# Two graph-attention layers on one core: layer-1 and layer-2 scores from extra weight columns, rows spread through DRAM, and a bfloat16 adjacency load

## The chip, the cores and the metric

The kernel runs on one core of a Trainium2 chip. Times are device microseconds (us) of that core. A profiled execution has a span (first to last instruction) and a time that also holds what lies around it.

## The reference

There are 32 samples, each with 512 nodes of 512 features and a 512x512 adjacency matrix of 0 and 1. Two blocks follow each other; each normalises the rows, applies ReLU, runs a graph attention and adds the result to its input.

```python
# layer 0 (one head): i attends to its neighbours j
s = s_src[i] + s_dst[j] + b;  e = leaky_relu(s, 0.2);  e = where(adj + eye == 0, -inf, e)
x = x + softmax(e, axis=j) @ h
# layer 1, gat_layer twice: 4 heads of 256, elu, then 1 head of 512
xl = x @ W;  asrc = einsum(xl, a_src);  adst = einsum(xl, a_dst)      # one number per node and head
e = leaky_relu(asrc[s] + adst[d], 0.2);  e = where(adj > 0 or s == d, e, -1e9)
out[d] = sum_s softmax(e, axis=s) * xl[s] + bias
```

Everything is computed in float32. In this text, layer 1 is the first `gat_layer` (four heads) and layer 2 the second (one head).

## The kernel before

A sample's 512 nodes are four tiles of 128 partitions (`T` = 4). All of a sample stays in SBUF. The program is written with tile pools; a scheduler decides the order of the instructions on each engine, and every engine runs its instructions in that order. A tile of a pool with `bufs` slots has to wait until the slot's last user is done.

An attention has these steps, and all of them appear in layer 0, in each of the four heads of layer 1 and in layer 2:

- **Projection** (`layer1_project`, L307; `layer2_project`, L383): products of 128 nodes by 512 columns, each accumulated over the contraction in PSUM, copied to SBUF by ACT (L311, L387). Layer 1 takes two heads at once.
- **Scores** (`dot`, L165): VectorE multiplies a row of features with an attention vector and sums, for source and target. The result is a column, one number per node: a and c.
- **Spread** (`spread`, L152): a column must lie along the free dimension, the same on all partitions. Four TensorE transposes, one per node tile, write it to a PSUM tile `row` of 128x512.
- **Maxima** (`neighbour_max`, L173): per node tile, VectorE adds the additive mask (0 or -2^100) to the row of a and takes the maximum. Then `shifts` works out, in tiny VectorE operations (L180 to L185), the two columns p and q. They contain the softmax's shift.
- **Edge weights** (`edge_weights`, L188 to L199): p and q are spread. Per node tile of 128x512: ACT computes q + 0.2 a (L195), VectorE max(p + a, that) (L196), POOL adds the mask (L197), ACT takes Exp (L198).
- **Aggregation** (`aggregate`, L206): TensorE multiplies the edge weights with the values and a column of ones, so that the sum of weights comes along. VectorE divides (L217 to L219, L345 to L346).

Layer 1's heads go through ELU (L352, L353) and are transposed for layer 2 (`layer1_head_T`, L366, L367).

The masks (`masks0`, `masks1`) come from the int32 adjacency tile on VectorE (L231 to L248), and are also transposed on TensorE (L160, L161). Layer 0's normalised rows are transposed in `layer1_in` (L160).

The main loop (L415) is software-pipelined: in step b it projects sample b for layer 1, aggregates layer 2 of sample b-1 (`layer2_out`), works out all four heads' maxima (`layer1_shifts`), then runs layer 0's aggregation of sample b+1 (`layer0_out`) and `layer1_in(b+1)`, the four heads of sample b with the next head's edge weights ahead of each, `layer2_project(b)`, and the masks, load and scores of samples b+1 and b+2. SP issues the loads of x and adj and the store of out; the constants are loaded from ACT's queue ahead of the loop. PSUM's eight slots are divided as `p_acc` 3, `p_tr` 2 and `p_bc` 3 (the rows).

Of the kernel before, what the change touches and what calls it, by code (L numbers as in the profile page):

```python
# [15 lines left out]
P = 128  # L16
# [8 lines left out]
def kernel(  # L25
# [32 lines left out]
    NW = 2 * H  # L58
# [13 lines left out]
    p_acc = ctx.enter_context(tc.tile_pool(name="p_acc", bufs=3, space=PSUM))  # L72
    p_tr = ctx.enter_context(tc.tile_pool(name="p_tr", bufs=2, space=PSUM))
    p_bc = ctx.enter_context(tc.tile_pool(name="p_bc", bufs=3, space=PSUM))
# [7 lines left out]
    def load_adj(b: int):  # L82
        A[b] = big.tile([P, T, N], I32, tag="adj", name=f"adj_{b}")
        nc.sync.dma_start(A[b], node_tiles(adj, b))
# [22 lines left out]
    w1_s = const.tile([P, KD, HF], F32, name="w1_s")  # L107
    w2_s = const.tile([P, KH, D], F32, name="w2_s")
    nc.scalar.dma_start(w1_s, w1.rearrange("(k p) f -> p k f", p=P))

    att1_r = const.tile([P, 2, HF], F32, name="att1_r")
    att2_r = const.tile([P, 2, D], F32, name="att2_r")
# [3 lines left out]
    def load_constants():  # L116
        for i, (a1, a2) in enumerate(((att_src1, att_src2), (att_dst1, att_dst2))):
            nc.scalar.dma_start(att1_r[:, i, :], rows(a1, HF))
            nc.scalar.dma_start(att2_r[:, i, :], rows(a2, D))
        nc.scalar.dma_start(b1_r, rows(b1, HF))  # L120
        nc.scalar.dma_start(b2_r, rows(b2, D))
        nc.scalar.dma_start(w2_s, w2.rearrange("(k p) f -> p k f", p=P))

        nc.vector.tensor_scalar(b1_r, b1_r, 1.0, None, op0=ALU.add)

# [22 lines left out]
    def spread(col_of):  # L148

        row = p_bc.tile([P, N], F32, tag="bc", name="row")  # L150
        for t in range(T):
            nc.tensor.transpose(row[:, node_block(t)], col_of(t).to_broadcast([P, P]), ident)  # L152
        return row
# [15 lines left out]
    def neighbour_max(amax, h, mask, row):  # L169

        for t in range(T):
            junk = work.tile([P, N], BF16, tag="junk", name="junk_m")
            nc.vector.tensor_tensor_reduce(  # L173
                junk, mask[:, t, :], row, 1.0, LOWEST, ALU.add, ALU.max, accum_out=amax[:, t, h : h + 1]
            )

    def shifts(c, amax, heads, name):

        z = cols.tile([P, T, heads], F32, tag=f"z{name}", name=f"z{name}")
        nc.vector.tensor_add(z, c, amax)  # L180
        m = cols.tile([P, T, heads], F32, tag=f"m{name}", name=f"m{name}")
        nc.vector.scalar_tensor_tensor(m, z, SLOPE, z, op0=ALU.mult, op1=ALU.max)  # L182
        pq = cols.tile([P, 2, T, heads], F32, tag=f"pq{name}", name=f"pq{name}")
        nc.vector.tensor_sub(pq[:, 0], c, m)
        nc.vector.scalar_tensor_tensor(pq[:, 1], c, SLOPE, m, op0=ALU.mult, op1=ALU.subtract)  # L185
        return pq

    def edge_weights(name, tag, pq, h, a_of, a2_of, mask):  # L188

        E = big.tile([P, T, N], F32, tag=tag, name=name, bufs=2)  # L190
        p_row = spread(lambda t: pq[:, 0, t, h : h + 1])
        q_row = spread(lambda t: pq[:, 1, t, h : h + 1])
        for t in range(T):
            e = E[:, t, :]
            nc.scalar.activation(e, q_row, AF.Identity, bias=a2_of(t), scale=1.0)  # L195
            nc.vector.scalar_tensor_tensor(e, p_row, a_of(t), e, op0=ALU.add, op1=ALU.max)  # L196
# [14 lines left out]
    def attend(E, values, xt):  # L211

        for t in range(T):
            hi = aggregate(E, t, lambda s: values[:, s, HD : D + 1])
# [9 lines left out]
    M = {}  # L224
# [30 lines left out]
    def layer0_scores(b: int):  # L255
# [4 lines left out]
        c = cols.tile([P, T, 1], F32, name="c0")  # L260
        a = cols.tile([P, T, 1], F32, name="a0")
        for t in range(T):
            relu_normed(h0[:, t, :D], xt, t, rstd, nmr)
            dot(h0[:, t, :D], ws_r, c[:, t, :])
            dot(h0[:, t, :D], wd_r, a[:, t, :])
        nc.vector.tensor_scalar(c, c, b0_r, None, op0=ALU.add)  # L266
        a2 = cols.tile([P, T, 1], F32, name="a20")
        nc.vector.tensor_scalar(a2, a, SLOPE, None, op0=ALU.mult)
        m0, m0T = masks0(b)
        amax = cols.tile([P, T, 1], F32, name="amax0")  # L270
        neighbour_max(amax, 0, m0, spread(lambda t: a[:, t, :]))
        pq = shifts(c, amax, 1, "0")
        L0[b] = (h0, edge_weights(f"E0_{b}", "E_one", pq, 0, lambda t: a[:, t, :], lambda t: a2[:, t, :], m0T))
# [23 lines left out]
    def layer1_project(b: int):  # L297
        hT = HT.pop(b)
        ac = cols.tile([P, T, NW], F32, name="ac1")

        xl = [big.tile([P, T, 2, F + 1], F32, tag="pair", name=f"xl_{b}_{i}", bufs=3) for i in range(PAIRS)]
        for i in range(PAIRS):
            nc.gpsimd.memset(xl[i][:, :, :, F : F + 1], 1.0)  # L303
            for t in range(T):
                acc = p_acc.tile([P, 512], F32, tag="acc", name="acc")
                for k in range(KD):
                    nc.tensor.matmul(  # L307
                        acc, hT[:, k, node_block(t)], w1_s[:, k, i * 512 : (i + 1) * 512],
                        start=(k == 0), stop=(k == KD - 1),
                    )  # L310
                nc.scalar.copy(xl[i][:, t, :, :F], acc.rearrange("p (h f) -> p h f", f=F))  # L311
                for j in range(2):
                    h = 2 * i + j
                    for side in range(2):
                        n = side * H + h
                        dot(xl[i][:, t, j, :F], att1_r[:, side, h * F : (h + 1) * F], ac[:, t, n : n + 1])
        L1[b] = (ac, xl)

    def layer1_shifts(b: int):
        ac, xl = L1[b]  # L320
        m1T = M[b][1]
        a2 = cols.tile([P, T, H], F32, name="a21")
        nc.vector.tensor_scalar(a2, ac[:, :, :H], SLOPE, None, op0=ALU.mult)
        amax = cols.tile([P, T, H], F32, name="amax1")
        for h in range(H):
            neighbour_max(amax, h, m1T, spread(lambda t: ac[:, t, h : h + 1]))
        pq = shifts(ac[:, :, H:], amax, H, "1")
        L1[b] = (ac, a2, pq, xl)
# [3 lines left out]
    def layer1_head_scores(b: int, h: int):  # L332
        ac, a2, pq, _ = L1[b]
        return edge_weights(
            f"E_{b}_{h}", "E", pq, h, lambda t: ac[:, t, h : h + 1], lambda t: a2[:, t, h : h + 1], M[b][0]
        )

    def layer1_head(b: int, h: int, E):

        xl = L1[b][3][h // 2]  # L340
        v = work.tile([P, T, F], F32, tag="v", name=f"v_{b}_{h}")
        for t in range(T):
            acc = aggregate(E, t, lambda s: xl[:, s, h % 2, :])
# [28 lines left out]
    def layer2_project(b: int):  # L372
# [4 lines left out]
        xl = big.tile([P, T, D + 1], F32, tag="xl2", name=f"xl2_{b}")  # L377
        nc.gpsimd.memset(xl[:, :, D : D + 1], 1.0)
        ac = cols.tile([P, T, 2], F32, name="ac2")
        for t in range(T):  # L380
            acc = p_acc.tile([P, 512], F32, tag="acc", name="acc")
            for k in range(KH):
                nc.tensor.matmul(  # L383
                    acc, h1T[k // per][:, k % per, node_block(t)], w2_s[:, k, :],
                    start=(k == 0), stop=(k == KH - 1),
                )
            nc.scalar.copy(xl[:, t, :D], acc)  # L387
            for side in range(2):
# [80 lines left out]
```

## Time and profile before

| | us |
|---|---|
| three runs | 4755.22, 4755.69, 4651.54 (median 4755.22) |
| the profiled execution, its time | 4652.77 |
| the profiled execution, its span | 4651.0 |
| TensorE busy with products | 4210.5 (91%) |
| VectorE busy | 2918.1 (63%) |
| ACT busy | 1841.0 (40%) |
| POOL busy | 1134.8 (24%) |

An fp32 product or transpose is one row of the program; a product's record in the trace is one of its two passes. In a row of the groups, the columns are: line, engine, operation, out<-in with shapes, count; then busy time in us and the mean in ns of one; then the idle time of the engine just before these instructions and what ended it. In a timeline the idle time stands in square brackets with what ended it. PEclk is the granted TensorE clock as a share of full speed. In the list of DMA issues, the last number is the median time from issue to landing, in us.

The chain of work that ended last gives 69% of the span to TensorE, 20% to VectorE, 4% to POOL and 4% to ACT.

### The profile page before, as it was taken

How to read it: one execution, taken by the hardware profiler on the slowest of the kernel's cores; microseconds unless marked ns; L12 is line 12 of the kernel's file. 1: busy time of each engine (PE TensorE's matmuls, PEld its weight loads, DVE VectorE, ACT ScalarE, POOL GpSimd, SP SyncE). 2: the span in 40 equal slices, each digit the busy share in tenths (PEclk: the TensorE clock that was granted, in tenths of full speed). 3: DMA queues.
4: the chain of work that ended last, by engine and by line, in shares of the span. 5: the costliest groups of instructions: out<-in, count | busy, mean ns of one | idle time of the engine just before them, and what ended most of it. 6: DMA issues, size and time to landing. Idle time of an engine off the chain costs nothing.

```text
span 4651.0 us, 49799 instructions
## 1 busy us (share of the span) xinstructions
PE 4210.5 (91%) x17152; PEld 2844.0 (61%) x17152; DVE 2918.1 (63%) x9029; ACT 1841.0 (40%) x3073; POOL 1134.8 (24%) x1094
## 2 busy tenths in 40 slices
PE   6998899898998989999889989899898999989997
PEld 4566656666565665656656566656566565665665
DVE  6656665567666576665666656766657666576644
ACT  2434324434344343343432444424434334343343
POOL 1322212223122232132321322212223213232121
PEclk9999999999999999999999999999999999999998
DMA  3000000000000000000000000000000000000000
GB/s 115 10 19 28 28 28 10 19 27 28 28 19 19 19 28 28 28 10 19 28 28 28 10 19 28 28 28 13 24 19 28 28 28 10 19 28 28 10 1 19
DMA packets 53802, 110.92 MB, mean 24 GB/s; under 512 B 1840, under 2 KB 1840, under 8 KB 53552
## 3 DMA queue, kind: packets, MB, share of 16 engines
q1 hardware_dynamic: 50688, 100.67, 6.2%
q10 hardware_dynamic: 2864, 7.08, 0.4%
q8 instruction: 137, 2.24, 0.2%
q14 instruction: 113, 0.93, 0.1%
HBM read 74.19 MB, written 33.55 MB: 23 GB/s over the span
## 4 chain that ended last, share of the span: by engine, by line
PE 69%; DVE 20%; POOL 4%; ACT 4%; issue 2%; DMA 0%; POOLq 0%; SPq 0%; ACTq 0%; DVEq 0%
PE acc L206 31%; PE acc L383 19%; PE acc L307 12%; DVE junk_m L173 7%; DVE junk L165 4%; POOL E L197 4%; DVE E L196 3%; PE pt L366 2%; PE pt L160 2%; ACT hn L146 2%; PE row L152 2%; DVE x L219 1%; DVE d L235 1%; POOL rstd L140 1%; DVE c L266 1%
## 5 line engine op out<-in xcount | busy, mean ns | idle before, releaser
L206 PE MATMUL acc<-xl,E 128*128 128x257 f32 (+1 forms) x6144 | 1420.0, 387 | 58.8 <-DVE v L346 53.3
L206 PEld LDWEIGHTS acc<-xl,E 128*128 128x128 f32 x6144 | 1158.3, 192 | 258.7 <-issue 72.4
L165 DVE SCALAR_TENSOR_TENSOR junk<-xl,att_r 128x256 bf16<-128x256 f32 (+1 forms) x1280 | 604.7, 524 | 765.4 <-ACT xl L387 750.1
L195 ACT ACTIVATE E<-row,a 128x512 f32<-128x512 f32 x768 | 478.8, 684 | 1256.3 <-PE row L152 1197.0
L197 POOL TENSOR_TENSOR E<-E,m 128x512 f32<-128x512 f32 x640 | 747.8, 1193 | 752.6 <-DVE E L196 750.3
L307 PE MATMUL acc<-w_s,hT 128*128 128x512 f32 x2048 | 922.3, 597 | 0.0
L383 PE MATMUL acc<-w_s,h1T 128*128 128x512 f32 x2048 | 894.8, 592 | 0.0
L383 PEld LDWEIGHTS acc<-w_s,h1T 128*128 128x128 f32 x2048 | 381.7, 190 | 443.9 <-issue 443.9
L206 PE MATMUL acc<-h,E 128*128 128x257 f32 (+1 forms) x2048 | 510.1, 408 | 134.1 <-DVE m L182 128.8
L196 DVE SCALAR_TENSOR_TENSOR E<-row,ac,E 128x512 f32<-128x512 f32 x640 | 452.0, 744 | 276.5 <-ACT E L195 276.4
L307 PEld LDWEIGHTS acc<-w_s,hT 128*128 128x128 f32 x2048 | 372.6, 191 | 385.3 <-issue 377.1
L198 ACT ACTIVATE E<-E 128x512 f32<-128x512 f32 x768 | 479.6, 628 | 272.6 <-POOL E L197 269.9
L206 PEld LDWEIGHTS acc<-h,E 128*128 128x128 f32 x2048 | 415.3, 207 | 209.3 <-issue 140.4
L173 DVE CUSTOM_DVE_ANT_0 junk_m<-m1T,row 128x512 bf16<-128x512 bf16 x640 | 394.1, 682 | 0.0
L387 ACT COPY xl<-acc 128x512 f32<-128x512 f32 x128 | 75.1, 587 | 741.2 <-PE acc L383 741.2
L219 DVE SCALAR_TENSOR_TENSOR x<-acc,r,x 128x256 f32<-128x256 f32 x512 | 246.4, 482 | 176.7 <-PE acc L206 169.4
L353 DVE SCALAR_TENSOR_TENSOR v<-e,v 128x512 f32<-128x512 f32 x256 | 178.1, 696 | 237.3 <-ACT e L352 237.3
L303 POOL MEMSET xl<- 128x8 f32 x64 | 7.1, 112 | 1053.1 <-PE acc L383 795.9
L152 PE MATMUL row<-ident,pq 128*128 128x128 f32 x1536 | 210.8, 278 | 43.2 <-ACT E L195 31.2
L140 POOL TENSOR_TENSOR rstd<-ve,minus_half 128x4 f32<-128x4 f32 x64 | 64.0, 1013 | 754.1 <-DVE ve L138 754.1
L311 ACT COPY xl<-acc 128x512 f32<-128x512 f32 x256 | 148.9, 582 | 244.4 <-PE acc L307 244.4
L346 DVE SCALAR_TENSOR_TENSOR v<-acc,r,b_r 128x256 f32<-128x256 f32 x512 | 238.9, 482 | 10.3
(64 smaller groups left out, 3262.1 us busy)
## 6 DMA issues: line engine op xcount, KB each, us to landing
x<-in_x_dram SPq DMA_DIRECT2D x32, 1024.0 KB, 5.1
adj<-in_adj_dram SPq DMA_DIRECT2D x32, 1024.0 KB, 5.2
out_dram<-x SPq DMA_DIRECT2D x32, 1024.0 KB, 4.3
w_s<-in_L_gnn_W_dram ACTq DMA_DIRECT2D x2, 2048.0 KB, 13.7
att_r<-in_L_gnn_att_src_dram ACTq DMA_DIRECT2D x1, 512.0 KB, 17.3
att_r<-in_L_gnn_att_dst_dram ACTq DMA_DIRECT2D x1, 512.0 KB, 7.4
b_r<-in_L_gnn_b_dram ACTq DMA_DIRECT2D x1, 512.0 KB, 9.5
ws_r<-in_L_gnn_attn_w_src_dram ACTq DMA_DIRECT2D x1, 256.0 KB, 5.2
```

Source lines behind the costliest of these rows:

```text
L152: nc.tensor.transpose(row[:, node_block(t)], col_of(t).to_broadcast([P, P]), ident)
L165: nc.vector.scalar_tensor_tensor(junk[:, : vector.shape[1]], values, 1.0, vector, op0=ALU.mult, op1=ALU.mult, accum_out=out)
L173: nc.vector.tensor_tensor_reduce(junk, mask[:, t, :], row, 1.0, LOWEST, ALU.add, ALU.max, accum_out=amax[:, t, h : h + 1])
L195: nc.scalar.activation(e, q_row, AF.Identity, bias=a2_of(t), scale=1.0)
L196: nc.vector.scalar_tensor_tensor(e, p_row, a_of(t), e, op0=ALU.add, op1=ALU.max)
L197: nc.gpsimd.tensor_add(e, e, mask[:, t, :])
L198: nc.scalar.activation(e, e, AF.Exp)
L206: nc.tensor.matmul(out, E[:, s, node_block(t)], values(s), start=(s == 0), stop=(s == T - 1))
L219: nc.vector.scalar_tensor_tensor(xt[:, t, f], acc[:, :HD], r, xt[:, t, f], op0=ALU.mult, op1=ALU.add)
L307: nc.tensor.matmul(acc, hT[:, k, node_block(t)], w1_s[:, k, i * 512 : (i + 1) * 512], start=(k == 0), stop=(k == KD - 1),)
L346: nc.vector.scalar_tensor_tensor(v[:, t, :], acc[:, :F], r, b1_r[:, h * F : (h + 1) * F], op0=ALU.mult, op1=ALU.add)
L383: nc.tensor.matmul(acc, h1T[k // per][:, k % per, node_block(t)], w2_s[:, k, :], start=(k == 0), stop=(k == KH - 1),)
```

## The change

Four things are edited.

1. The weights of layer 1 and layer 2 get two more columns per head, W times a_src and W times a_dst. They are worked out once on VectorE, in the prologue. The projection then yields a and c itself, so the dots over the projected rows are gone. Layer 1's projection is now one head per product (258 columns); layer 2's is two products of 257 columns.
2. `spread` no longer transposes a broadcast column per tile into PSUM. One transpose turns the 4 columns of a (or the 8 of p and q) into 4 (8) partitions, ACT copies them to SBUF, SP stores them to a DRAM tile, and SP loads them from there onto all 128 partitions. The row tiles are now in SBUF, two slots for a and two for p with q. PSUM's slots are redivided as `p_acc` 5 and `p_tr` 3.
3. adj is loaded as bfloat16 by POOL's DMA queue, in place of int32 by SP's.
4. `layer1_project` and `layer1_shifts` go head by head, each head's shifts (with its maxima) behind the next head's projection. The last head's shifts stand behind `layer2_out`. `layer0_out(b+1)` and `layer1_in(b+1)` are moved from ahead of the heads to behind them.

The core of the diff:

```diff
-    p_acc = ctx.enter_context(tc.tile_pool(name="p_acc", bufs=3, space=PSUM))
-    p_tr = ctx.enter_context(tc.tile_pool(name="p_tr", bufs=2, space=PSUM))
-    p_bc = ctx.enter_context(tc.tile_pool(name="p_bc", bufs=3, space=PSUM))
+    p_acc = ctx.enter_context(tc.tile_pool(name="p_acc", bufs=5, space=PSUM))
+    p_tr = ctx.enter_context(tc.tile_pool(name="p_tr", bufs=3, space=PSUM))
+    dram = ctx.enter_context(tc.tile_pool(name="dram", bufs=4, space=bass.MemoryType.DRAM))
...
     def load_adj(b: int):
-        A[b] = big.tile([P, T, N], I32, tag="adj", name=f"adj_{b}")
-        nc.sync.dma_start(A[b], node_tiles(adj, b))
+        A[b] = big.tile([P, T, N], BF16, tag="adj", name=f"adj_{b}")
+        nc.gpsimd.dma_start(A[b], node_tiles(adj, b))
...
+        for h in range(H):
+            for k in range(KD):
+                for i in range(2):
+                    dot(w1_s[:, k, h, 2:], att1_r[:, i, h * F : (h + 1) * F], w1_s[:, k, h, i : i + 1])
+        for k in range(KH):
+            for i in range(2):
+                dot(w2_s[:, k, 2:], att2_r[:, i, :], w2_s[:, k, i : i + 1])
...
-    def spread(col_of):
-        row = p_bc.tile([P, N], F32, tag="bc", name="row")
-        for t in range(T):
-            nc.tensor.transpose(row[:, node_block(t)], col_of(t).to_broadcast([P, P]), ident)
+    def spread(col, n, tag, bufs):
+        pt = p_tr.tile([P, N], F32, tag="tr", name="pt_row")
+        nc.tensor.transpose(pt[: n * T, :P], col, ident)
+        line = cols.tile([n * T, P], F32, tag=f"line{n}", name="line")
+        nc.scalar.copy(line, pt[: n * T, :P])
+        there = dram.tile([n * T, P], F32, tag=f"there{n}", name="there")
+        nc.sync.dma_start(there, line)
+        row = big.tile([P, n, N], F32, tag=tag, name=tag, bufs=bufs)
+        nc.sync.dma_start(row, there.rearrange("r p -> (r p)").partition_broadcast(P).rearrange("q (n m) -> q n m", n=n))
         return row
...
+    def shift_rows(a, c, mask):
+        a_row = spread(a, 1, "a_row", 2)
...
+        neighbour_max(amax, mask, a_row[:, 0, :])
...
+        return a2, spread(pq.rearrange("p r t -> p (r t)"), 2, "pq_row", 2)
...
-            nc.scalar.activation(e, q_row, AF.Identity, bias=a2_of(t), scale=1.0)
-            nc.vector.scalar_tensor_tensor(e, p_row, a_of(t), e, op0=ALU.add, op1=ALU.max)
+            nc.scalar.activation(e, rows_pq[:, 1, :], AF.Identity, bias=a2[:, t : t + 1], scale=1.0)
+            nc.vector.scalar_tensor_tensor(e, rows_pq[:, 0, :], a[:, t : t + 1], e, op0=ALU.add, op1=ALU.max)
             nc.gpsimd.tensor_add(e, e, mask[:, t, :])
             nc.scalar.activation(e, e, AF.Exp)
...
+    def layer1_project(b: int, h: int):
...
+                nc.tensor.matmul(
+                    acc[:, : 2 + F], HT[b][:, k, node_block(t)], w1_s[:, k, h, :],
...
+            nc.scalar.copy(xl[:, t, h % 2, : 2 + F], acc[:, : 2 + F])
...
+            accs = [p_acc.tile([P, 512], F32, tag="acc", name="acc") for _ in range(2)]
             for k in range(KH):
...
+                for i in range(2):
+                    nc.tensor.matmul(
+                        accs[i][:, :W], h1T[k // per][:, k % per, node_block(t)], w2_s[:, k, i * W : (i + 1) * W],
...
         if b < B:
-            layer1_project(b)
+            for h in range(H):
+                layer1_project(b, h)
+                if h:
+                    layer1_shifts(b, h - 1)
...
-        layer1_shifts(b)
-        if b + 1 < B:
-            layer0_out(b + 1)
-            layer1_in(b + 1)
+        layer1_shifts(b, H - 1)
...
         layer1_head_T(b, H - 1)
+        if b + 1 < B:
+            layer0_out(b + 1)
+            layer1_in(b + 1)
         layer2_project(b)
```

## The prediction

> **What bounds the kernel now.** I read the table of stages over one sample first (from one layer-2 aggregation at 1949.00 us to the next at 2092.36), then TensorE's timeline inside it, then the groups by shape.
>
> ```profile
> core 0: us, PE busy (x) PEld busy (x) DVE busy (x) ACT busy (x) POOL busy (x), PEclk, DMA share, GB/s
> 1949.00:2092.36 143.36, 131.11 (x538) 88.63 (x537) 91.22 (x283) 57.45 (x96) 35.49 (x34) 0.98 0.06 23
> ```
>
> 32 periods of 143.36 us make 4587.5 of the 4651.0 us span; 63.5 us lie ahead and behind. TensorE is busy 131.1 us of a period and idle 12.25, in a few waits:
>
> ```profile
> 1973.90 10.35 PE L206 MATMUL acc<-h,E 128*128 128x256 f32 x40 [4.11 <-DVE m L182]
> ...
> 1988.19 0.44 PE L160 MATMUL pt<-ident,hn 128*128 128x128 f32 x2 [2.63 <-ACT hn L146]
> ...
> 2073.09 0.65 PE L160 MATMUL pt<-ident_b,m 128*128 128x128 bf16 x8 [1.99 <-DVE m L236]
> ```
>
> So TensorE sets the time, and the others are late in places. The prices:
>
> ```profile
> L206 PE MATMUL acc<-xl,E 128*128 128x257 f32 x5120 | 1214.4, 388 | 58.8 <-DVE v L346 53.3 <-ACT E L198 3.6 <-DVE r L345 0.5
> L197 POOL TENSOR_TENSOR E<-E,m 128x512 f32<-128x512 f32 x640 | 747.8, 1193 | 752.6 <-DVE E L196 750.3 <-DVE r L345 1.0
> L195 ACT ACTIVATE E<-row,a 128x512 f32<-128x512 f32 x768 | 478.8, 684 | 1256.3 <-PE row L152 1197.0 <-DVE junk L165 59.3
> L196 DVE SCALAR_TENSOR_TENSOR E<-row,ac,E 128x512 f32<-128x512 f32 x640 | 452.0, 744 | 276.5 <-ACT E L195 276.4
> L165 DVE SCALAR_TENSOR_TENSOR junk<-xl,att_r 128x256 bf16<-128x256 f32 x1024 | 437.8, 483 | 15.3 <-ACT xl L311 15.2
> L173 DVE CUSTOM_DVE_ANT_0 junk_m<-m1T,row 128x512 bf16<-128x512 bf16 x640 | 394.1, 682 | 0.0
> L152 PE MATMUL row<-ident,pq 128*128 128x128 f32 x1536 | 210.8, 278 | 43.2 <-ACT E L195 31.2 <-DVE pq L185 7.3 <-DVE pq L184 4.7
> ```
>
> Durations overlap at their edges, so I take start-to-start paces: in the chain in order of time 64 passes of a 257-column product take 13.86 us (0.2166 each; an fp32 product is two passes), 60 of 512 columns 25.77 (0.4295), 8 transposes 0.87 (0.109). In the timeline four maxima step 0.61 us, edge-weight combinations 0.65 behind a first of 0.74, three POOL adds take 3.40 (1.13 each), ACT passes step 0.61 to 0.63.
>
> Transfers: the issues and the queue.
>
> ```profile
> x<-in_x_dram SPq DMA_DIRECT2D x32, 1024.0 KB, 5.1
> ...
> out_dram<-x SPq DMA_DIRECT2D x32, 1024.0 KB, 4.3
> ...
> ws_r<-in_L_gnn_attn_w_src_dram ACTq DMA_DIRECT2D x1, 256.0 KB, 5.2
> ```
>
> The queue row gives 50688 packets at 6.2% of 16 engines: 0.062 x 16 x 4651 / 50688 = 91 ns per 2 KB packet, so 1 MB (32 packets per engine) moves in 2.9 us, and 2.2 us of a load and 1.4 us of a store are fixed.
>
> **The change, part by part.**
>
> *Weight columns.* TensorE per sample: 64 passes of 512 columns (27.5 us) become 128 of 258 (0.2174 from the two paces: 27.8), and 64 more become 128 of 257 (27.7): +0.6 us. VectorE loses the dots, (437.8 + 167.0 + 99.6)/32 = 22.0 us a sample. 48 dots over the weights (32 of 0.5, 16 of 0.69: 27 us) come once, ahead of the first projection.
>
> *Spreads.* 72 transposes a sample (7.85 us) become 12 (1.3): -6.5 us. TensorE's net is -5.9 us a sample, 190 us in all. What takes their place is a chain: transpose, ACT copy of a 4- or 8-row line, store to DRAM, SP's wait for it, load on 128 partitions. The ACT copy lies between 0 and the 0.58 us of a 128x512 one; I take 0.25. The store: at least one packet, 0.1, at most the 4.3 of a 1 MB store; I take the fixed 1.4 and a packet, 1.5. The loads (256 KB for a, 512 KB for p and q): at least 2.2, at most 5.2 to 17.3 (the prologue's constants, which queue behind each other); I take 2.2 + 8 or 16 packets: 2.9 and 3.7. A round trip is thus 4.4 or 5.2 us, where eight transposes took 0.87. The Trainium skill, "DMA: Bandwidth & Descriptors", section "Anatomy of one DMA", puts the fixed part at about 2.0 us and the rest at bytes over 436 GB/s: by it a trip would be 4.6 and 5.2, so the sum would stay.
>
> *Rows in SBUF.* The combination and the maximum now have two SBUF inputs (before, the row came from PSUM). Here is what that does beside a POOL add, in the timeline of layer 2's edge weights:
>
> ```profile
> 2066.20 0.69 DVE L165 SCALAR_TENSOR_TENSOR junk<-h,ws_r 128x512 bf16<-128x512 f32 x1
> ...
> 2067.64 4.95 POOL L197 TENSOR_TENSOR E<-E,m 128x512 f32<-128x512 f32 x4 [12.99 <-DVE E L196]
> ...
> 2069.45 1.01 DVE L165 SCALAR_TENSOR_TENSOR junk<-h,wd_r 128x512 bf16<-128x512 f32 x1
> ...
> 2070.39 1.11 DVE L266 TENSOR_SCALAR c<-c,b_r 128x4 f32<-128x4 f32 x1
> ```
>
> The dot with two SBUF inputs takes 0.69 us alone and 1.01 among POOL's adds, which slow from 1.13 to 1.24 each; L266 needs 0.22 in the prologue and 1.11 here. So I let combinations, maxima and adds take turns. Bounds: no effect, or full exclusion; I take exclusion, because these rows fit it. The Trainium skill, "SBUF — State Buffer", section "Who interferes with whom", states it as an exclusive lock between a GpSimd instruction that reads SBUF and a VectorE instruction with two SBUF inputs. By that rule the sum is the one below; were it wrong here, rival (2).
>
> *Where the spreads stand.* The order built for each engine decides. Per sample of the steady state:
>
> ```
> PE   a(L2) after product 1 of 64; pq(L2) after 23; masks; a(L0) after 30; pq(L0), a(h0) after 62;
>      29 products of layer2_out, pq(h0), a(h1), 3 more; per head h: 4 of 16 products, pq(h+1), a(h+2), 12;
>      layer0_out; layer2_project with the transposes of hn among it
> DVE  per head: first combination, 4 maxima of head h+1, three combinations among z, m, pq of h+1, v
> ACT  per head: 4 identities, 4 Exp, and only then the line copies of pq(h+1), a(h+2)
> SP   per head: store pq, store a, load pq, load a; out(b-1) stands ahead of the load of pq(h0), x(b+2) behind a(h1)
> ```
>
> So head h+1's maxima start behind head h's pq, and its pq line waits on ACT for head h's last Exp. That is a loop, from one pq landing to the next: identity and first combination 1.45; four maxima with POOL's first add among them 2.45 + 1.13 = 3.6 (5.0); second combination 0.7 (5.7); then adds and combinations by turns, three adds of 1.18 and two of 0.7, 4.95 (10.7); Exp 0.65, line 0.3 (11.65); trip and issue 5.35: **17.0 us per head**, where TensorE has 7 us of products. A second loop runs through TensorE: 11.35 + 11 products (4.77) + r and v (0.9) = 17.0, and v stands ahead of the next first combination on VectorE, 0.7 us of slack. The clock spoils that: after an idle stretch it is half,
>
> ```profile
> 1962.69 1.47 PE L152 MATMUL row<-ident,ac 128*128 128x128 f32 x12
> ```
>
> against 2.79 us for 12 such transposes at 4549.86, behind a wait of 7.31 us. All 11 products at half clock add 4.8; I take 1.5, less the slack: 17.8.
>
> *The period*, from the first projection product of a sample at 0. a(L2): copies of the last halves 1.2, transpose and line 1.75, landed 6.2, maxima 8.7, z, m, pq among three dots 10.9; TensorE's 22 products (9.6) cover it. pq(L2) lands at 16.9; the masks' copies hold ACT until 18.2; first combination 19.6, three more and four adds by turns 6.5 (26.1), Exp 26.75. The line of a(L0) is queued behind these Exps on ACT: 27.0, landed 31.6, maxima 34.1, small ones and the next mask 35.6; TensorE came at 32.2 and waits 3.4. pq(L0), a(h0): lines 36.4, landed 41.6, combination 43.1, by turns 49.6, maxima 52.0, small ones 53.5; TensorE came at 49.3, waits 4.2. pq(h0): line 54.3, stored 55.8; the 1 MB store of out is issued just ahead of the load: landed between 59.7 and 62.6, I take 61.2. Three head loops: 61.2 + 53.4 = 114.6. The last head: 1.5 + 6.5 + 0.6, 11 products 4.8, layer0_out and transposes 15 (28.4), layer2_project 27.7, transposes of hn 2.9, a wait for hn 1.5 (60.5), half clock after gaps 2 (62.5). **Period 177.1**, 34 more than now.
>
> layer0_out and layer1_in moved behind the heads, so they no longer fill the heads' waits; they cover the last v's transposes. x(b+2) and the adj load, now on POOL's queue behind layer 2's adds, are waited for by the mask at 35: issued near 27, bounds 5.1 and 13.7 (the 2 MB weights), from no cost to 5 us; I take none. POOL's next adds come at 43, so nothing is queued behind it. Masks from bfloat16 cost no more than the 1.21 us of int32.
>
> Sum: 32 x 177.1 = 5667; ahead and behind 63.5 + 30 (weight dots 20, two trips in the last layer 2 10): 5761; outside the span 1.8 (4652.77 - 4651.0): **5763, say 5760 us**. The profiled execution (4652.8) is the lowest of the three shown; the median, 4755.2, lies 2.2% above it.
>
> **Rivals.** (1) *TensorE's saving decides* (faster): 4652 - 190 = 4460. For it: VectorE is relieved by 22 us a sample and the waits at L182 and L146 could shrink. It needs the head loop to fit in TensorE's 7 us; without any trip it is 11.65. Only trips of 2 us on average (eight on the path, 34 us to win back) would end level. (2) *No taking turns, full clock, out not in the way*: head loop 14.4, period 158, 5150. (3) *Trips like the prologue's*, 2 us longer: +16 us, period 193, 6270. (4) *adj lands late*: +5 us, 5920.
>
> **How the numbers follow.** Forecast with (4), 5500 to 6050: 0.47. Towards (2), 4750 to 5500: 0.25. Towards (3), above 6050: 0.16. (1): 0.08; near level, as the trips at their lower bound: 0.04. A measurement tells about 2% from no change: faster 0.08, same 0.04, slower 0.88. Range 5050 to 6350, the bounds of (2) and (3) with 2% to either side; it leaves out (1), the level case and some 0.08 of the tails. The forecast's own is 5500 to 6050.
>
> **What would show it.** Right: waits of 5 us and more on TensorE at the first product of each head, released by ACT's Exp; identities waiting for a DMA of the pq row four to six times a sample; first product of head to head 17 to 18 us apart; POOL's adds above 1.2 us. Wrong: heads under 10 us apart, or a period under 143 with the waits gone; then the trips are shorter than I took or the chains overlap. A pq row landing 3.5 us after its issue or sooner, with heads still 17 apart, would put the cause on VectorE and POOL instead.

## The result and the profile after

The changed kernel takes 5727.5 us (median of four runs, 5720.9 to 5732.2). The kernel before takes 4651.1 and 4651.5 us beside it, and the ratio is 1.231 (95% interval 1.229 to 1.234): slower by 23%. Executions of before near 4755 us, and of the kernel with adj alone near 4761, in which TensorE's granted clock was 0.94 instead of 0.97, are left out of every comparison below, except in experiment 10, where every execution of that experiment's kernel comes near them.

The page of the kernel after (span 5729.6 us): the engines' busy time and the shares of the chain of work that ended last.

```profile
PE 4493.5 (78%) x19328; PEld 3585.7 (63%) x19328; DVE 2859.4 (50%) x7045; ACT 2011.1 (35%) x3841; POOL 1401.5 (24%) x1126
...
PE 48%; DVE 24%; DMA 11%; POOL 9%; ACT 5%; issue 3%; SPq 0%; ACTq 0%; POOLq 0%
```

TensorE was busy 91% of the span before; now it is 78%. Its busy time rose by 283 us although it has fewer transposes to do; the mean granted clock fell from 0.973 to 0.855. The table of stages over one sample, from one first projection product to the next (columns as in the prediction's first table):

```profile
2550.20:2727.70 177.50, 140.88 (x606) 112.30 (x605) 88.61 (x217) 62.75 (x121) 43.86 (x35) 0.85 0.14 42
```

A sample takes 177.5 us where it took 143.4. What TensorE and ScalarE wait for, in the list of waits (total us, times, longest us):

```profile
PE acc L225 <- ACT E L217: 876.5, 350, 11.7
ACT E L214 <- DMA pq_row<-there: 471.3, 129, 9.9
```

The aggregation products (L225) wait for the Exps of their head (L217), and the heads' first identities (L214) for the row of p and q: 129 times in 32 samples, four a sample. The groups by shape (busy us, mean ns of one, then the idle time ahead of them and its releaser):

```profile
L216 POOL TENSOR_TENSOR E<-E,m 128x512 f32<-128x512 f32 x640 | 939.0, 1484 | 2093.7 <-DVE E L215 1843.0 <-DVE z L201 250.7
L215 DVE SCALAR_TENSOR_TENSOR E<-pq_row,xl,E 128x512 f32<-128x512 f32 x640 | 669.2, 1071 | 324.9 <-ACT E L214 323.9
...
L203 DVE SCALAR_TENSOR_TENSOR m<-z 128x4 f32<-128x4 f32 x192 | 121.2, 631 | 0.2
```

The add and the combination took 1193 and 744 ns before, and the maxima went from 682 to 916. L203 works on four elements per partition and yet has a mean of 631 ns.

### The profile page after: what moved, and what is told of

Read it like the earlier page. It is cut to its first block, busy times and chain, and to the rows that moved or that the text cites. A ratio compares the mean times of both kernels' runs of the same rounds, so it can differ in the third digit from the quotient of the medians.

```text
span 5729.6 us, 53608 instructions
## 1 busy us (share of the span) xinstructions
PE 4493.5 (78%) x19328; PEld 3585.7 (63%) x19328; DVE 2859.4 (50%) x7045; ACT 2011.1 (35%) x3841; POOL 1401.5 (24%) x1126
## 4 chain that ended last, share of the span: by engine, by line
PE 48%; DVE 24%; DMA 11%; POOL 9%; ACT 5%; issue 3%; SPq 0%; ACTq 0%; POOLq 0%
PE acc L225 24%; PE acc L390 14%; DVE junk_m L189 10%; POOL E L216 9%; DVE E L215 8%; PE acc L324 7%; DMA pq_row<-there 6%; DMA a_row<-there 3%; PE pt L371 2%; ACT E L217 2%; PE pt L176 2%; DMA there<-line 1%; DVE m L203 1%; ACT E L214 1%; ACT hn L156 1%
## 5 line engine op out<-in xcount | busy, mean ns | idle before, releaser
L225 PE MATMUL acc<-xl,E 128*128 128x257 f32 (+1 forms) x6144 | 1892.9, 468 | 867.6 <-ACT E L217 867.4
L225 PEld LDWEIGHTS acc<-xl,E 128*128 128x128 f32 x6144 | 1387.6, 235 | 1322.6 <-ACT E L217 1092.0
L216 POOL TENSOR_TENSOR E<-E,m 128x512 f32<-128x512 f32 x640 | 939.0, 1484 | 2093.7 <-DVE E L215 1843.0
L324 PE MATMUL acc<-w_s,hT 128*128 128x258 f32 x4096 | 961.1, 389 | 42.7 <-ACT xl L328 42.7
L390 PE MATMUL acc<-w_s,h1T 128*128 128x257 f32 x4096 | 916.4, 379 | 0.0
L324 PEld LDWEIGHTS acc<-w_s,hT 128*128 128x128 f32 x4096 | 771.7, 193 | 165.2 <-ACT xl L328 55.3
L217 ACT ACTIVATE E<-E 128x512 f32<-128x512 f32 x768 | 483.8, 630 | 1008.2 <-POOL E L216 1008.1
L390 PEld LDWEIGHTS acc<-w_s,h1T 128*128 128x128 f32 x4096 | 766.0, 189 | 107.6
L215 DVE SCALAR_TENSOR_TENSOR E<-pq_row,xl,E 128x512 f32<-128x512 f32 x640 | 669.2, 1071 | 324.9 <-ACT E L214 323.9
L214 ACT ACTIVATE E<-pq_row,a 128x512 f32<-128x512 f32 x768 | 491.5, 714 | 473.9 <-DMA pq_row<-there 471.3
L189 DVE CUSTOM_DVE_ANT_0 junk_m<-m1T,a_row 128x512 bf16<-128x512 bf16 x640 | 552.6, 916 | 164.5 <-DMA a_row<-there 164.5
L225 PE MATMUL acc<-h,E 128*128 128x257 f32 (+1 forms) x2048 | 463.9, 381 | 11.4 <-ACT E L217 9.1
L225 PEld LDWEIGHTS acc<-h,E 128*128 128x128 f32 x2048 | 382.2, 191 | 65.3 <-ACT E L217 11.6
L216 POOL TENSOR_TENSOR E<-E,m0T 128x512 f32<-128x512 f32 x128 | 200.4, 1593 | 614.1 <-DVE E L215 614.1
L238 DVE SCALAR_TENSOR_TENSOR x<-acc,r,x 128x256 f32<-128x256 f32 x512 | 244.8, 479 | 202.3 <-PE acc L225 196.4
```

Of the source, the lines that this page charges most:

```text
L189: nc.vector.tensor_tensor_reduce(junk, mask[:, t, :], row, 1.0, LOWEST, ALU.add, ALU.max, accum_out=amax[:, t : t + 1])
L214: nc.scalar.activation(e, rows_pq[:, 1, :], AF.Identity, bias=a2[:, t : t + 1], scale=1.0)
L215: nc.vector.scalar_tensor_tensor(e, rows_pq[:, 0, :], a[:, t : t + 1], e, op0=ALU.add, op1=ALU.max)
L216: nc.gpsimd.tensor_add(e, e, mask[:, t, :])
L217: nc.scalar.activation(e, e, AF.Exp)
L225: nc.tensor.matmul(out, E[:, s, node_block(t)], values(s), start=(s == 0), stop=(s == T - 1))
```

## Inside a head of the kernel after

First TensorE's timeline at the start of three of the four heads of a sample (start, us, what, and in brackets the idle time ahead of it):

```profile
2618.08 2.94 PE L225 MATMUL acc<-xl,E 128*128 128x257 f32 x6 [11.05 <-ACT E L217]
...
2634.66 2.94 PE L225 MATMUL acc<-xl,E 128*128 128x257 f32 x6 [3.71 <-ACT E L217]
...
2653.44 2.40 PE L225 MATMUL acc<-xl,E 128*128 128x257 f32 x6 [3.71 <-ACT E L217]
```

The heads start 16.6 and 18.8 us apart, and the fourth 16.5 us behind the third, for 6.9 us of products. Six passes take up to 2.94 us, where the pace of before makes 1.3: about half the pace after each idle stretch (the granted clock from 2618 to 2622 us is 0.50). Next the chain that ended last, from the landing of head 0's row to that of head 1 (start, us, what):

```profile
2608.12 6.04 DMA pq_row<-there
2614.24 0.73 ACT E L214
...
2616.36 1.55 DVE junk_m L189
...
2620.54 1.03 DVE m L203
2621.57 1.65 DVE E L215
...
2625.28 1.22 DMA there<-line
2626.52 3.70 DMA pq_row<-there
```

Read downwards, it is the prediction's first loop: identity, combination, head 1's maxima, its small steps, the adds and combinations by turns, the line, the trip. Head 0's load took 6.04 us, that of head 1 3.70; ahead of head 0's the 1 MB store of out (L404) was issued on the same queue at 2607.62. VectorE's pieces of 1.55, 1.03 and 1.65 us are the turns. In POOL's timeline one add begins at 2615.83, and two, one behind the other and 2.78 us together, at 2619.89: the pieces stand beside these adds.

## The experiments

The prediction took the order of the trips as given, priced a trip at 4.4 to 5.2 us, and let VectorE and POOL take turns. The first four kernels ask which of the three holds the 1076 us that the change lost; the others follow from their answers.

**1. Spreads by TensorE, the rest of the change kept.** The 72 transposes a sample, four for each of 18 rows, return (three PSUM slots for rows, three for products, two for transposes); columns, order of the loops and adj stay as in the kernel after.

```
-        pt = p_tr.tile([P, N], F32, tag="tr", name="pt_row")
-        nc.tensor.transpose(pt[: n * T, :P], col, ident)
...
+        for i in range(n):
+            row = p_bc.tile([P, N], F32, tag="bc", name="row")
+            for t in range(T):
+                j = i * T + t
+                nc.tensor.transpose(row[:, node_block(t)], col[:, j : j + 1].to_broadcast([P, P]), ident)
```

> The changed kernel with the rows spread as before (four transposes per column into PSUM, p_acc 3, p_tr 2, p_bc 3); weight columns, bfloat16 adj and the new order of the loop stay. No trips, no rows in SBUF. My theory (trips and rows in SBUF are the loss): TensorE has 121 + 6.5 us of work a sample and waits of some 10: period 135 to 145, 4400 to 4700 us. Rival (the new order of the loop, layer0_out behind the heads, is the loss): 5100 us or more.

Measured: 4328.1 us, 0.931 of before (0.929 to 0.932), better than expected and faster than both kernels. Its page (span 4326.1 us):

```profile
PE 4127.5 (95%) x21248; PEld 3510.4 (81%) x21248; DVE 2452.0 (57%) x7045; ACT 1902.5 (44%) x3457; POOL 1164.2 (27%) x1126
```

So the whole loss, 1399 us against this kernel, comes with the spreads through DRAM (and the PSUM slots that go with them), and the other parts of the change together are a gain of 7%. TensorE runs more instructions here than before the change (21248 against 17152, most of them narrower) in 83 us less busy time, at a clock of 0.997.

**2. The same, with the rows copied to SBUF.** ScalarE copies each row from PSUM to SBUF (18 copies a sample), and the copies are read.

```
+            nc.scalar.copy(out[:, i, :], row)
```

> As e1_tensor_spread, but ACT copies each spread row from PSUM to an SBUF tile (18 copies of 0.6 us a sample), so that VectorE's combinations and maxima have two SBUF inputs as in the changed kernel. No trips. My theory: turns between VectorE and POOL cost 1.5 to 2.5 us per set of edge weights, six sets a sample, and ACT's copies add to the chain: 3 to 10% above e1_tensor_spread; POOL's adds at 1.4 us or more. Rival (taking turns is covered): within 2% of e1_tensor_spread.

Measured: 5069.8 us, 1.09 of before (1.088 to 1.092), and 17% above the first kernel where 3 to 10% were expected. Two things are in it, the copies and the place that is read.

**3. The same copies, read by nobody.** The readers stay in PSUM.

```
+            spare = big.tile([P, N], F32, tag=f"spare_{tag}", name="spare", bufs=bufs)
+            nc.scalar.copy(spare, row)
```

> The kernel with TensorE spreads, whose rows ScalarE copies to SBUF as in the run at 5070 us, but nothing reads the copies: VectorE and ScalarE still read the rows in PSUM. If that run's 741 us were the turns between VectorE and POOL, this one stays near 4328: 4330 to 4500 us, and POOL's add at 1.2 us. Rival: the 741 us were ScalarE's 576 extra copies ahead of the edge weights: 4900 us or more.

Measured: 4439.0 us, 0.954 of before (0.952 to 0.956). The copies cost 111 us, the place of the rows 631 (5070 - 4439, 19.7 us a sample), without any DMA in the spreads. The combination's group in the kernel that reads SBUF:

```profile
L213 DVE SCALAR_TENSOR_TENSOR E<-pq_row,xl,E 128x512 f32<-128x512 f32 x640 | 627.6, 1017 | 245.3 <-ACT E L212 241.1
```

and of the one whose copies are unread:

```profile
L215 DVE SCALAR_TENSOR_TENSOR E<-row,xl,E 128x512 f32<-128x512 f32 x640 | 455.6, 742 | 56.1 <-ACT E L214 50.0
```

The combination grows from 742 to 1017 ns and POOL's add, in the group beside it, from 1207 to 1424 when the row is in SBUF. This agrees with the Trainium skill, "SBUF — State Buffer", section "Who interferes with whom", which says that a VectorE instruction with two SBUF inputs contends with a GpSimd instruction that reads SBUF. The order built for the engines also differs between the two kernels, and TensorE's granted clock is 0.938 in the one and 0.997 in the other (busy 4420.9 and 4154.6 us), so part of the 631 us can be a consequence of that.

**4. An extra hop in each trip.** The kernel after, with one more transfer from DRAM to DRAM between store and load.

```
+        there2 = dram.tile([n * T, P], F32, tag=f"again{n}", name="again")
+        nc.sync.dma_start(there2, there)
```

> The changed kernel with every trip made longer by one more hop, DRAM tile to DRAM tile, between the store and the load. My theory: eight trips a sample stand on the path; a hop takes some 2 us (between the 1.2 of a store and the 3.6 of a load in the trace), so 16 us a sample more: 6240 us (6040 to 6650). Rival (trips are mostly covered by VectorE, POOL and the half clock): under 5880 us.

Measured: 5874.7 us, 1.263 of before (1.261 to 1.265): 147 us more, 4.6 us a sample, where eight trips in series would have added 16: the rival's side (under 5880), and a miss of the expected 6240. The hop's transfer takes 1.8 to 2.7 us where it was looked at. The chain that ended last, over one head:

```profile
2693.07 0.72 ACT e L359
2693.79 0.62 ACT E L216
...
2703.92 0.64 ACT E L219
2704.60 5.84 PE acc L227 x22
2711.25 0.72 ACT e L359
```

No DMA is among its pieces, those left out included: from one head's identity (L216) to the next the time goes through edge weights, Exp, products and the e of head h, which stands ahead of the next identity on ScalarE. Beside the trips' loop there is a second one through TensorE, and it takes 18.2 us here. A longer trip is hidden in it. The order moved too: head 0's trip now starts behind all products of layer2_out, and the store of out is issued while the hop runs. SP, which waits 91.1 us in all for that store's x in the kernel after, waits 27.5 us here, so the 4.6 us are net of some 2 us a sample that this saves.

**5. Own PSUM slots for the transposes.** In the kernel after, the transposes of a, of pq, of hn, of the masks and of v share three PSUM buffers under one tag. In the built order they stand in the order of the program: head h+1's row of a cannot pass head h's row of pq. Here a and pq have a slot each, the other transposes two, and the products four instead of five; rows still go through DRAM and lie in SBUF.

```
-    p_acc = ctx.enter_context(tc.tile_pool(name="p_acc", bufs=5, space=PSUM))
-    p_tr = ctx.enter_context(tc.tile_pool(name="p_tr", bufs=3, space=PSUM))
+    p_acc = ctx.enter_context(tc.tile_pool(name="p_acc", bufs=4, space=PSUM))
+    p_tr = ctx.enter_context(tc.tile_pool(name="p_tr", bufs=2, space=PSUM))
...
-        pt = p_tr.tile([P, N], F32, tag="tr", name="pt_row")
+        pt = p_tr.tile([P, N], F32, tag=f"tr{n}", name="pt_row", bufs=1)
```

> The changed kernel with one edit to its PSUM slots: the transposes of a and those of p with q get a slot of their own each (p_acc 4, p_tr 2), so that the spread of a(h+1) no longer has to be placed behind that of pq(h). Trips, rows in SBUF and all else stay. My theory (the eight trips stand one behind the other on the path because the shared slot orders the spreads): in the built order the spreads of a and pq of heads 0 to 2 move into the projection and layer2_out, the head loops of 16 to 19 us fall to what POOL and VectorE need by turns (some 8 us), and the period falls from 177.5 to 140 to 150 us: 4600 to 4900 us. Rival (a trip costs its latency wherever it stands, or the taking of turns between VectorE and POOL sets the heads): 5400 us or more.

Measured: 4868.5 us, 1.047 of before (1.045 to 1.048): 859 us won back. TensorE's timeline:

```profile
2505.77 0.27 PE L162 MATMUL pt_row<-ident,pq 128*8 128x128 f32 x1 [0.30 <-DVE pq L206]
2505.88 1.47 PE L324 MATMUL acc<-w_s,hT 128*128 128x258 f32 x6
...
2563.27 1.04 PE L371 MATMUL pt<-ident,v 128*128 128x128 f32 x8
...
2573.33 1.03 PE L371 MATMUL pt<-ident,v 128*128 128x128 f32 x8
```

The rows of pq now start among the projection's products (L324) and layer2_out's, well ahead of their heads, and two heads' v (L371) are 10.1 us apart, the pair before 11.5. TensorE's wait for the heads' Exp falls from 876.5 to 190.6 us. The turns are untouched: 1494 ns for POOL's add, 1180 for the combination.

**6. The extra hop in the kernel with own slots.** Both edits together.

> The kernel with own slots (4868 us) with one more transfer from DRAM to DRAM in each trip (1.7 to 2.1 us each by the run with the hop). If with own slots the trips lie beside other work: at most 100 us more, 4870 to 4970 us. Rival: most of a sample's trips stand in series on the path here too: 8 trips by 2.0 us by 32 samples, 512 us, so 5200 us or more.

Measured: 5051.6 us, 1.086 of before (1.084 to 1.088): 183 us more than with own slots alone, 5.7 us a sample. It lies between the two expectations, nearer to the trips being covered: of the 16 us a sample that the expectation gives eight hops, about a third is on the path.

**7. All landed rows copied to PSUM.** The kernel after with its trips; ScalarE copies each row from SBUF to PSUM, and all readers read there (PSUM slots 3, 2 and 3).

```
+            ps = p_bc.tile([P, N], F32, tag="bc", name="row_ps")
+            nc.scalar.copy(ps, row[:, i, :])
```

> The kernel after with its DMA trips, but ScalarE copies each landed row into PSUM (18 copies a sample), so that VectorE's maxima and edge weights have one SBUF operand as before; PSUM pools as before the change (3, 2, 3). If VectorE and POOL taking turns over SBUF is a third or more of the loss, POOL's add falls from 1.48 to about 1.2 us, VectorE's edge weight from 1.07 to about 0.75, and the time to 4900 to 5450 us in spite of the copies. Rival: trips and their order are all of the loss and the turns none; then the copies (0.59 us each, 576 of them) come on top: 5700 us or more.

Measured: 5066.9 us, 1.089 of before (1.087 to 1.091), inside the range of the first theory: 661 us less than after, in spite of 576 more copies. POOL's add takes 1155 ns, the combination 742. Since the order of the trips moved with the edit, not all of it is the turns'.

**8. Both cures.** Own slots and all rows in PSUM; for want of PSUM the transposes of v and of the masks are left with one slot and the rows with two.

> The kernel after with its DMA trips, with both cures: own PSUM slots for the transposes of a and of pq, and rows copied from SBUF to PSUM before VectorE reads them (PSUM slots: acc 3, transposes 1, a 1, pq 1, rows 2). If the fixed order (859 us) and the turns of VectorE and POOL (631 us by two runs that differ only in where the rows are read) are the loss, and the trips themselves lie beside other work, then 4440 to 4640 us, the POOL add at 1.2 us. Rival: a trip's own time still stands in the way when the order no longer forces it: 4800 us or more.

Measured: 5408.9 us, 1.163 of before (1.161 to 1.166): slower than either cure alone, and a miss of the expectation. The add is at 1155 ns and the combination at 744, so the turns are gone; but with one slot the transposes of v wait for v and for the copy of the pair before them, inside every head:

```profile
2649.79 0.64 PE L377 MATMUL pt<-ident,v 128*128 128x128 f32 x2 [2.04 <-DVE v L364]
2651.22 1.11 PE L377 MATMUL pt<-ident,v 128*128 128x128 f32 x4 [0.78 <-ACT h1T L378]
```

These two waits make 268.5 us in all. TensorE's largest wait is still that for the heads' Exp (L223), 490.7 us where experiment 5 has 190.6: with two slots for the rows, those of p and q take both, and ScalarE copies the next head's row of a only behind them (p and q at 2632.16, a at 2636.58), so an order is forced here too. The run says nothing on the trips, because the cure took away slots that were needed, and what each of them costs is not separated.

**9. Own slots, and only p in PSUM.** One PSUM bank for p, filled by ScalarE; a and q are read in SBUF, products have three slots instead of four.

```
+        p_row = p_bc.tile([P, N], F32, tag="bc", name="p_row")
+        nc.scalar.copy(p_row, rows_pq[:, 0, :])
...
-            nc.vector.scalar_tensor_tensor(e, rows_pq[:, 0, :], a[:, t : t + 1], e, op0=ALU.add, op1=ALU.max)
+            nc.vector.scalar_tensor_tensor(e, p_row, a[:, t : t + 1], e, op0=ALU.add, op1=ALU.max)
```

> The kernel with own slots (4868 us), where ScalarE copies the p half of each landed row to one PSUM bank (6 copies a sample, 0.58 us each), so that VectorE's edge weight has one SBUF operand; the maxima and q are still read in SBUF. PSUM slots: acc 3 instead of 4, and 1 for p. It takes up the run with both cures, which had only one slot left for the transposes of v and did not answer. If the turns of VectorE and POOL carry most of the 540 us between own slots and TensorE spreads: the edge weight falls from 1.18 to about 0.75 us, the POOL add from 1.49 to about 1.3, the time to 4500 to 4720 us. Rival: the rest is the trips' own time or the copies eat the gain, 4820 us or more.

Measured: 4572.4 us, 0.982 of before (0.981 to 0.984). All trips through DRAM are kept, and the kernel is faster than before. Its groups:

```profile
L218 DVE SCALAR_TENSOR_TENSOR E<-p_row,xl,E 128x512 f32<-128x512 f32 x640 | 443.5, 741 | 199.1 <-ACT E L217 115.4 <-ACT p_row L214 83.7
L190 DVE CUSTOM_DVE_ANT_0 junk_m<-m1T,a_row 128x512 bf16<-128x512 bf16 x640 | 502.2, 834 | 326.3 <-DMA a_row<-there 326.2
```

The combination is back at its price of before, and so nearly is the add with 1205 ns; the maxima, which still read SBUF, are not. 296 us won by an edit that adds 112 us of copies.

**10. Only the weight columns.** The kernel before, with nothing but the columns.

> Only the score columns are taken over; rows, adj, loop order and PSUM pools are those of before. My reading: the columns take the layer-1 and layer-2 dot products off VectorE and make the projections 16% wider on TensorE, which paces the kernel before (131.1 of 143.4 us a sample). So a small gain: 4450 to 4600 us. Rival: the gain of the kernel with TensorE spreads over before (4328 against 4652) is the new order of the loops and not the columns; then 4630 us or more here.

Measured: 4765.2 us, 1.025 of before (1.023 to 1.027): no gain, and the rival's side. (The projections are 0.8% wider, 258 columns for 256, and not 16%.) The tables of stages, first before the change, the stretch of the maxima of all heads and the products behind it:

```profile
1963.00:1974.00 11.00, 6.89 (x40) 5.87 (x38) 11.00 (x39) 0.00 (x0) 0.08 (x1) 0.98 0.52 191
1974.00:1984.00 10.00, 10.00 (x40) 8.56 (x41) 7.81 (x24) 0.00 (x0) 0.00 (x0) 0.86 0.01 2
```

then with the columns, the same two stretches (the clock is the third number from the end):

```profile
2013.50:2024.50 11.00, 6.89 (x41) 5.87 (x39) 11.00 (x39) 0.00 (x0) 0.10 (x1) 0.94 0.54 192
2024.50:2036.10 11.60, 11.60 (x42) 9.70 (x43) 8.01 (x24) 0.00 (x0) 0.00 (x0) 0.76 0.01 1
```

and last the products behind the same wait in the profiled execution of experiment 11's kernel, 4761.8 us, which has no columns:

```profile
2022.60:2034.40 11.80, 11.74 (x42) 9.80 (x43) 8.08 (x24) 0.00 (x0) 0.00 (x0) 0.75 0.00 1
```

VectorE lost 488 us of work (2918 to 2430 busy), but in the stage where TensorE waits for it, it does the same 11.00 us: those are the 16 maxima, not the dots. The half clock behind that wait lasted longer in this kernel, 0.76 over the 40 products, where it was 0.86 in the profile of before. The columns are not needed for that: without them it was 0.75 in the execution at 4761.8 us. So 4765 belongs beside the executions without columns at 4755 to 4762 us, from which it differs by 3 to 10 us, and the 114 us are not shown to be the columns' price. What sets how long the half clock lasts is not settled.

**11. Only adj as bfloat16.** The kernel before with the converting load on POOL's queue.

> Only the load of adj is changed (converted to bfloat16 on the way, issued on POOL's queue). My reading: the mask operations of VectorE become a little shorter and lie beside TensorE's work, the load lands long before it is read: within 1% of before, 4600 to 4660 us. Rival: the converting load, or its 0.8 us of issue on POOL ahead of an edge-weight add, delays a head: 4700 us or more.

Measured: 4657.5 us in a single execution, 0.15% above before's 4650.7. The load costs and brings nothing that shows.

**12. The old place of layer0_out and layer1_in.** The first kernel (4328 us), with these two ahead of the heads again.

```
-        if b + 1 < B:
-            layer0_out(b + 1)
-            layer1_in(b + 1)
         layer2_project(b)
```

> The kernel with TensorE spreads (4328 us), but layer0_out and layer1_in of the next sample stand ahead of the heads again, as before; the maxima stay behind each head's projection. The columns alone gave no gain (4765 against 4651), so the 7% must come from the order. In before, one sample has TensorE idle for some 4 us behind the maxima of all heads and for some 3.5 us behind the layer norm of layer1_in, and half clock after each (0.85 to 0.86 for some 20 us). My reading: both halves of the order bring about equal parts: 4450 to 4560 us here. Rivals: the place of layer0_out brings nothing, 4370 us or less; or it brings all, 4630 us or more.

Measured: 4350.8 us, 0.935 of before (0.933 to 0.937), 23 us above the first kernel: the place of layer0_out brings half a per cent, a miss of the expected half share. This kernel is the one of experiment 10 with the shifts worked out head by head behind the projections, that is the maxima, the small steps and the spreads of p and q (and with the adj load, worth nothing). So that brings the rest: 4765 to 4351, of which some 100 us may be the longer half clock of experiment 10; against 4651 it is 300, the columns included. The table of stages, from the products of layer0_out on (length, TensorE's busy time, and so on):

```profile
2525.00:2542.00 17.00, 16.65 (x79) 14.19 (x78) 12.86 (x43) 0.23 (x1) 1.56 (x2) 1.00 0.35 124
```

There is no stretch of 4 us without products any more, and the half clock behind it is gone with it: 1.00 from the projections to the heads.

The way from one kernel to the next, each step the difference of two measured times:

| from | to | step | us |
|---|---|---|---|
| before, 4651 | 4765 | weight columns alone | +114 |
| 4765 | 4351 | maxima and shifts behind each head's projection, adj | -414 |
| 4351 | 4328 | layer0_out, layer1_in behind the heads | -23 |
| 4328 | 4572 | rows through DRAM, own slots, p read in PSUM | +244 |
| 4572 | 4868 | p read in SBUF | +296 |
| 4868 | after, 5727 | one PSUM tag for all transposes | +859 |

The first two rows share the doubt of experiment 10; their sum, -300, does not. The fastest is the kernel with all of the change but the spreads through DRAM: 4328 us, 7.0% below before.

## Why the prediction was right, and where it was not

The forecast was 5760 us, the time 5727, for the reasons given; the period was 177.5 us against 177.1. Its terms:

- *Three head loops*, 53.4: from one head's first identity to the next 16.0, 17.3 and 18.5, together 51.8. From head 1 on the chain that ended last goes through TensorE's products (7.47 us for 22 passes at 2642.27), so the loop through TensorE takes over.
- *The way to head 0's row*, 61.2: its first identity came at 64.0 (2614.24 - 2550.2). Up to head 0's line the sum holds: ScalarE begins it at 2604.33, 54.1 us into the period, where 54.3 was taken. What it lacks is a wait on SP: the store of out, ahead of the row's load, needs the last x of layer 2 (L238) and is issued at 2607.62, 3.0 us behind the store of the line (2604.61), which takes 1.15 to 1.22. The load behind it took 6.04.
- *From head 3's row to the next period*, 62.5: 61.7.
- *A trip*: line 0.25 as taken, store 1.15 to 1.22 for 1.5, load of pq for the heads behind head 0 3.6 to 3.7 for 3.7. The load of layer 0's a took 5.18 for 2.9; the adj load, issued on POOL's queue at 2574.87, runs beside it. The Trainium skill, "DMA: Bandwidth & Descriptors", section "Anatomy of one DMA", gives about 2.0 us fixed for its GpSimd path; these small stores on SP's queue landed in less.
- *TensorE's waits* at the masks 3.4 and in layer2_out 4.2: 3.63 and 3.44.
- *Ahead of and behind the periods*, 93.5: 5729.6 - 32 x 177.5 leaves 49.6. This was the worst term, too large by 44, and it makes up for the period's shortfall of 0.4 x 32 = 13 and more. That the sum came within 1% is in part luck: the errors, +2.8, -1.6 and -0.8 us in a sample and -44 at the ends, have different signs.
- *Taking turns* is shown by experiments 2, 3 and 9. The rival without them and with a full clock stood 19 us a sample below the forecast; reading rows in SBUF alone costs 19.7 in the pair of experiments 2 and 3. That the two numbers are so close need not mean more, since that rival also gives up the half clock and the store of out, and the pair differs in order and clock too.
- *The signs*: the heads' pitch (16.5 to 18.8 us), identities that wait for the row four times a sample, and POOL's adds of 1.48 us came. The wait of 5 us and more on TensorE came at head 0 only (11.05); the other three heads wait 3.71, 3.71 and 2.73 us, and there the chain goes through TensorE's own products, as said above.
- *Two slips* change nothing: the lowest of the three runs shown is 4651.54 us, not the profiled 4652.8, and 2% above rival (3) is 6395, not 6350.

The step that failed is "Only trips of 2 us on average (eight on the path, 34 us to win back) would end level", and with it rival (3), where trips 2 us longer cost 16 us a sample. The hop made the trips about that much longer and cost 4.6, net of the 2 us that it saved on SP. The eight trips are on the path only in part: once a head loop is as long as 17 us, the loop through TensorE, 17.8 in the prediction's own working, is just as long and hides what the trip adds. And level does not need trips of 2 us: with trips of 5 us and more, experiment 9 ends 1.8% below before. What made the trips dear was the order, in which each head's trip began only when the head before it was half done. The prediction wrote this order down, and took it as part of the trips' price; it is an effect of one shared PSUM tag, and the largest single step of the table. The prediction also gave VectorE's 22 us of dots no gain, which experiment 10 bears out, and had no term for the maxima behind each head's projection, which with the columns brings 300 us (4651 to 4351) when the rows are spread by TensorE.

What stays open: how the 244 us between the kernels of 4572 and 4328 us divide between the trips, the maxima that still read SBUF, and ScalarE's copies. They are net of the 60 transposes a sample that TensorE no longer does (6.5 us a sample by the prediction's working), so the trips themselves may cost more than 244 us.

## What to carry to other kernels

When a step becomes long in latency, ask first how early it can be issued: buffers that it shares with others under one tag fix its place in the order, and here two slots of their own were worth 859 us, more than three times the 244 us that part the best kernel with the transfers from the one without. Keep one operand of a VectorE instruction in PSUM where POOL is reading SBUF beside it: that was worth 296 us in experiment 9. Work taken off an engine counts only in the stage where someone waits for that engine: here 488 us less on VectorE brought nothing.

## What was not expected of the hardware

- A VectorE instruction of four elements per partition with two SBUF inputs (L203) took 1.11 us at 2620.47 in the kernel after, beside a POOL add that had begun at 2619.89, and 0.16 us at 2603.12, with no add beside it. Over 192 of them the mean is 631 ns in the kernel after and 175 ns in that of experiment 5, whose order is another.
- A wait of 4 us costs TensorE more than its length. Behind the 4.11 us ahead of layer0_out in the kernel before, 40 passes ran at a granted clock of 0.86 (0.76 and 0.75 in the profiles of experiments 10 and 11). In the kernel of experiment 12, without that wait, the mean over the span is 0.997, where it is 0.973 before.
- Storing 2 or 4 KB to DRAM, as a row of 4 or 8 partitions, landed in 1.15 to 1.22 us at most places on the chain of the kernel after; in that of experiment 5 a store issued 1.6 us behind the load of a row of a took 5.05 us (2648.23). The copy from DRAM to DRAM of the same size took 1.8 to 2.7 in experiment 4.
